# A four-layer graph network: one-hot spans of 128 nodes at multiples of 64, a ring of 44 chunks, and scores tied to a product

## The chip, the core and the metric

The kernel runs on one core of a Trainium2 chip. The metric is the device time of one execution in microseconds; three runs of the kernel before gave 4579.54, 4588.5 and 4594.84 us, so the median is 4588.5 us. The profile is of one further execution.

## What is computed

3125 nodes with 256 features pass four layers. Each adds the result of a graph step and of a dense mixer to the nodes, and then of a mixture of experts. The graph steps sum rows of their neighbours. 50000 edges, sorted by destination, serve layers 0, 1 and 3; layer 2 sums by the other end of the edge. The last mixture of experts has an attention over 32768 edges of its own.

```python
# layer 0 (layer 3 alike, without the relation types)
msgs = where(edge_type == r, x[src] @ rel_W[r], msgs)        # r = 0..3
agg  = segment_sum(msgs, dst);  deg = clip(segment_sum(1, dst), 1)
out  = relu(x @ self_W + self_b + agg / deg)
# layer 1: attention with 4 heads over the edges (the last experts' gates alike)
att   = leaky_relu(s_src[src] + s_dst[dst] + e_proj, 0.2)
exps  = exp(att - segment_max(att, dst)[dst])
alpha = exps / (segment_sum(exps, dst)[dst] + 1e-12)
out   = segment_sum(x_proj[src] * alpha, dst) + bias
# layer 2
agg   = segment_sum(A_values * h[col], row)
```

## The kernel before

**Chunks, tiles and one-hots.** Nodes lie in 25 tiles of 128. The 50000 edges lie in 391 chunks of 128, sorted by destination, so a tile takes about 16 chunks. For each chunk POOL issues an indirect DMA that gathers 128 rows of a table (L447, L842). DVE makes a one-hot matrix `E` from the edges' places `dl` (L416, L418): row = edge, column = node. PE multiplies it with the gathered rows and adds the result up in a PSUM tile `seg` (L430). `near` (L48) gives the tiles that chunk c may touch: one in the middle of a tile, two within three chunks of a boundary. A chunk with two tiles gets a one-hot of 256 columns and two products, one for each tile's own accumulator. After a tile's last product its `close` reads the sum from PSUM. The kernel first checks that the edges keep to these bounds (`regular`, L2370, and `route_check`, L2086, for the last attention); if they don't, a general path is taken instead.

**Gather loops.** `seg_near` (L434) serves layers 0, 2 and 3: gathers go to a ring of 16 buffers, and the products of chunk i - 12 are emitted after gather i. Layer 2 weights its one-hots. `gat_near` (L782) serves layer 1 and the tail. It has one ring of 35 chunks. Softmax works on batches of 16 chunks: `batch` adds gathered and stored scores (L806), takes running maxima over equal destinations along the edges (transposes by PE into `ga`, scans by DVE, L812 to L829), and writes `ex` by an exponential on ACT (L834). A batch starts 8 chunks after its last gather, and chunk i - 30 is scaled in place by `ex` (L854, DVE) and multiplied after gather i. A gather waits until the product of the chunk that had its buffer is done.

**What runs beside it.** Generators are interleaved by `drive`: three chunks of layer 0 to a step of its mixer, four of layer 1 to one step of its mixer, one of the layernorm and two of the edge scores, two of layer 3 to a step of its mixer, four of the tail to three steps of the experts. Within this a scheduler orders PE, DVE, ACT and SP at compile time; POOL keeps the order of emission. [...] 

**Names.** `mm` (L107) is the helper for dense products, `ps` takes a PSUM bank, `l1_edge_scores` (L1353) adds edge scores to `pre`, `gat_close` (L859), `l0_close` (L1027) and `l3_close` (L1755) finish a tile. `hb` (L1794) is the layernorm of layer 3's mixer.

Of the kernel before, what the change touches and what calls it, by code (L numbers as in the profile page):

```python
# [7 lines left out]
F32 = mybir.dt.float32  # L8
BF16 = mybir.dt.bfloat16
I32 = mybir.dt.int32  # L10
AF = mybir.ActivationFunctionType
# [24 lines left out]
AHEAD = 12  # L36
HALO = 40
CB = 16
RING = 35
T2 = 16  # L40
BIG = 2.0 ** 100

# [5 lines left out]
def near(c, nt=T):  # L48


    return range(max(0, (c - 3) >> 4), min(nt - 1, (c + 3) >> 4) + 1)


def lin_size(n):
# [10 lines left out]
def drive(*gens):  # L65

    live = list(gens)
    while live:
        for g in list(live):
            for _ in range(g[1]):  # L70
                try:
                    next(g[0])
                except StopIteration:
                    live.remove(g)
                    break
# [19 lines left out]
class Net:  # L95
    def __init__(self, tc, a, out):
        self.tc, self.nc, self.a, self.out = tc, tc.nc, a, out
        self.flip = 0
        self.apart = {}
        self.one_hots = 8  # L100
        self.pump = None


    def ps(self, n=512, name="mm", parts=P):
# [2 lines left out]
    def mm(self, out, pairs):  # L107
        last = len(pairs) - 1
        for i, (l, r) in enumerate(pairs):
            m = self.nc.tensor.matmul(out, l, r, start=(i == 0), stop=(i == last))  # L110
            if self.pump is not None:
                self.pump.after(m.ins, out.free_size())

# [308 lines left out]
    def to_tiles(self, pool, g, c, rows_c, A, w, close, weight=None):  # L422


        for t, e in self.one_hot(pool, g, c, weight):
# [5 lines left out]
            if last:  # L431
                close(t, A.pop(t))

    def seg_near(self, pool, g, table, gidx, close, count=False, ahead=AHEAD, weight=None):  # L434


        nc = self.nc
        n = g["n"]
        w = D + count
        ring = [pool.tile([P, w], F32, name=f"G{i}") for i in range(ahead + 4)]  # L440
        if count:
            for r in ring:
                nc.vector.memset(r[:, D:], 1.0)
        A = {}
        for i in range(n + ahead):
            if i < n:
                nc.gpsimd.indirect_dma_start(out=ring[i % len(ring)][:, :D], out_offset=None, in_=table,  # L447
                                             in_offset=bass.IndirectOffsetOnAxis(ap=gidx[:, i:i + 1], axis=0))
            c = i - ahead
            if c >= 0:  # L450
                self.to_tiles(pool, g, c, ring[c % len(ring)], A, w, close, weight)
            yield

    def table_sum(self, pool, ts, t0, n, out):
# [324 lines left out]
            v = pre[:, q * per:(q + 1) * per, :]  # L779
            self.evac(v, ps[q].rearrange("p (h c) -> p c h", h=4))  # L780

    def gat_near(self, pool, g, table, pre, pen, d, close):  # L782

        nc = self.nc
        n, late = g["n"], CB + 14
        f = d + 2
        nb = -(-n // CB)  # L790
        ring = pool.tile([P, RING, 4, f], F32, name="ring")
        att = pool.tile([P, nb * CB + 2, 4], F32, name="att")
        ex = pool.tile([P, nb * CB, 4], F32, name="ex")
        nc.vector.memset(att, 0.0)

        def spans(c0, c1):
            while c0 < c1:
                e = min(c1, c0 - c0 % RING + RING)
                yield c0, e, ring[:, c0 % RING:c0 % RING + e - c0]
                c0 = e  # L800

        def batch(b):
            c0 = b * CB
            lo, hi = (c0 + 1 if b else 0), min(c0 + CB + 1, n)
            for s, e, r in spans(lo, hi):
                nc.vector.tensor_add(att[:, s + 1:e + 1, :], r[:, :, :, d + 1], pre[:, s:e, :])  # L806
            v = att[:, lo + 1:hi + 1, :]
            nc.vector.scalar_tensor_tensor(v, v, 0.2, v, op0=OP.mult, op1=OP.max)
            yield
# [21 lines left out]
            qv = q.rearrange("p (j c h) -> p j c h", j=2, h=4)  # L831
            dif = pool.tile([P, CB, 4], F32, name="dif", bufs=2)
            nc.vector.tensor_sub(dif, att[:, c0 + 1:c0 + CB + 1, :], qv[:, 0])
            nc.scalar.activation(ex[:, c0:c0 + CB, :], dif, AF.Exp)  # L834
            for s, e, r in spans(c0, min(c0 + CB, n)):
                nc.vector.tensor_copy(r[:, :, :, d + 1], qv[:, 1, s - c0:e - c0, :])

# [1 line left out]
        live = []  # L839
        for i in range(n + late):  # L840
            if i < n:
                nc.gpsimd.indirect_dma_start(out=ring[:, i % RING].rearrange("p h f -> p (h f)"), out_offset=None,  # L842
                                             in_=table,
                                             in_offset=bass.IndirectOffsetOnAxis(ap=g["src"][:, i:i + 1], axis=0))
            for b in range(nb):
                if i == min(b * CB + CB, n - 1) + 8:
                    live.append(batch(b))
            for s in list(live):
                if next(s, self) is self:
                    live.remove(s)  # L850
            c = i - late
            if c >= 0:
                r = ring[:, c % RING]
                nc.vector.tensor_mul(r[:, :, :d + 1], r[:, :, :d + 1],  # L854
                                     ex[:, c, :, None].to_broadcast([P, 4, d + 1]))
                self.to_tiles(pool, g, c, r.rearrange("p h f -> p (h f)"), A, 4 * f, close)
            yield

    def gat_close(self, pool, table, d, aself, nodeg, eps, out):  # L859
# [1226 lines left out]
    def route_check(self, pool, table, ok):  # L2086

        nc = self.nc
        rec = self.load_all(pool, "rec6", table, 2)
        bad = pool.tile([P, 5], F32, name="rc_b")  # L2090
        nc.vector.memset(bad, 0.0)
        nc.vector.tensor_copy(bad[:, 4:5], self.beyond)
        dst = pool.tile([P, C2], F32, name="rc_d")
        far = pool.tile([P, C2], F32, name="rc_f")
        nc.vector.tensor_copy(dst, rec[:, :, 1])
        self.ordered(pool, dst, C2, self.dlin2, bad[:, 0:2])

        lo = self.first_nodes(pool, self.sixteenths(pool, "rc13", 13, C2))
        hi = self.first_nodes(pool, self.sixteenths(pool, "rc19", 20, C2))
        nc.vector.tensor_tensor(far, dst, lo, op=OP.is_lt)  # L2100
        nc.vector.tensor_reduce(bad[:, 2:3], far, axis=AX.X, op=OP.add)
        nc.vector.tensor_scalar(hi, hi, 128.0, float(T2 * P), op0=OP.add, op1=OP.min)
        nc.vector.tensor_tensor(far, dst, hi, op=OP.is_ge)
        nc.vector.tensor_reduce(bad[:, 3:4], far, axis=AX.X, op=OP.add)
        self.none_bad(pool, bad, ok)

    def l3_near_setup(self, keep, pool, table, penc):
# [4 lines left out]
        g["src"] = keep.tile([P, C2], I32, name="e2src")  # L2112
        g["dl"] = keep.tile([P, C2], F32, name="e2dl")
        nc.vector.tensor_copy(g["src"], rec[:, :, 0])
        nc.vector.tensor_sub(g["dl"], rec[:, :, 1], self.first_nodes(pool, self.sixteenths(pool, "ns", 13, C2)))
        w = self.load(pool, "wg", wtile(a["L3_ffn_W_gat"]))
        full = [P, T, 16]
        h = pool.tile(full, F32, name="h")
# [121 lines left out]
    def tail_regular(self, sorted_r):  # L2240
# [3 lines left out]
        with tp("g3") as gp, tp("ffn3") as fp, Banks(self, mm=4, ga=2, seg=2):  # L2244
# [21 lines left out]
                if t % 4 == 3:  # L2266
                    gate(t - 3, 4)
            close = self.gat_close(gp, rows_d, 4, aself, nodeg, 1e-16, out)
            drive((self.gat_near(gp, g, rows_d, pre, pen, 4, close), 4), (experts, 3))

    def tail_general(self):
        nc, tc, a = self.nc, self.tc, self.a
# [41 lines left out]
    def first_nodes(self, pool, lim):  # L2314

        v = pool.tile([P, lim.shape[1]], F32, name="lo128")
        self.nc.vector.tensor_scalar(lim, lim, 1.0, 1.0, op0=OP.max, op1=OP.subtract)
        self.nc.vector.tensor_scalar(v, lim, 128.0, None, op0=OP.mult)
        return v

    def ordered(self, pool, dstf, n, dlin, bad):

# [47 lines left out]
    def regular(self, pool, g):  # L2370


        nc = self.nc
        full = [P, C1]
        lim = [self.sixteenths(pool, f"rg_{base}", base) for base in (13, 3)]
        tf = self.bits(pool, g["dst"], "rg_t", 7)
        junk = pool.tile(full, F32, name="rg_j")
        bad = pool.tile([P, 5], F32, name="rg_b")
        nc.vector.memset(bad, 0.0)
        nc.vector.scalar_tensor_tensor(junk, tf, 1.0, lim[0], op0=OP.add, op1=OP.is_lt, accum_out=bad[:, 0:1])  # L2380
        nc.vector.scalar_tensor_tensor(junk, tf, 0.0, lim[1], op0=OP.add, op1=OP.is_gt, accum_out=bad[:, 1:2])
        self.dlin = self.dramk.tile([1, lin_size(C1)], F32, name="dlin")
        self.ordered(pool, g["dstf"], C1, self.dlin, bad[:, 2:4])

        self.sbase = self.keep.tile([P, T], F32, name="sbase")
        self.counts(pool, self.bits(pool, g["src"], "rg_k", 7), C1, T, self.sbase)
        self.uneven(pool, self.sbase, T, bad[:, 4:5])
        ok = pool.tile([P, 1], I32, name="rg_ok")
        self.none_bad(pool, bad, ok)

        g["dl"] = self.keep.tile(full, F32, name="e1dl")
        nc.vector.tensor_sub(g["dl"], g["dstf"], self.first_nodes(pool, lim[0]))
        return ok

    def fast(self):
# [3 lines left out]
        with tc.tile_pool(name="keepf", bufs=1) as keep, tc.tile_pool(name="dramf", bufs=1, space=DRAM) as dram:  # L2399
# [1 line left out]
            tp = lambda name: tc.tile_pool(name=name, bufs=1)  # L2401
            plain = dict(mm=6, acc=2)
            edges = dict(mm=3, acc=2, g=3)
            sums = dict(mm=3, acc=2, seg=3)


            self.deg2 = keep.tile([P, T], F32, name="deg2")
# [33 lines left out]
            with tp("att1") as gp:  # L2441
# [9 lines left out]
                def add_x(t, o):  # L2451
                    v = self.x[:, t, :].rearrange("p (h f) -> p h f", h=4)
                    nc.vector.tensor_add(v, v, o)
                    closed.add(t)
                with Banks(self, mm=1, acc=2, ga=2, seg=3), tp("mix1") as mp:
                    close = self.gat_close(gp, table, 64, aself, nodeg, 1e-12, add_x)
                    drive((self.gat_near(gp, g, table, pre, pen, 64, close), 4), (self.l1_mix_lean(mp), 1),
                          (self.norm_after(closed, self.mixed), 1), (self.l1_edge_scores(mp, pre, vb), 2))
            with Banks(self, **plain):
                route = tp("route")  # L2460
# [336 lines left out]
```

## Time and profile before

| | |
|---|---|
| median of three runs | 4588.5 us |
| the profiled execution | 4591.9 us |
| its span, first to last instruction | 4590.2 us |
| granted TensorE clock, mean | 0.859 |
| seg products of L430, `G` | 3210 records, 917.6 us busy |
| seg products of L430, `ring` | 1762 records, 424.5 us busy |
| one-hots of L416 | 1173, 365.1 us busy |

A product of fp32 stands in the trace as two records, so 4972 records are 2486 products: 535 for each of layers 0 to 3 and 346 in the tail. [...] the mean length of one record is longer than the time until the next starts. A row of the page's groups gives busy time, the mean of one, and the idle time of the engine before such instructions with its releasers. `G<-h_tab` are the gathers of layer 0, `ring<-l1rows` of layer 1, `G<-tab,e3src` of layer 2, `G<-tab,e1src` of layer 3, and `ring<-l3rows` of the tail.

### The profile page before, as it was taken

How to read it: one execution, taken by the hardware profiler on the slowest of the kernel's cores; microseconds unless marked ns; L12 is line 12 of the kernel's file. 1: busy time of each engine (PE TensorE's matmuls, PEld its weight loads, DVE VectorE, ACT ScalarE, POOL GpSimd, SP SyncE). 2: the span in 40 equal slices, each digit the busy share in tenths (PEclk: the TensorE clock that was granted, in tenths of full speed). 3: DMA queues.
4: the chain of work that ended last, by engine and by line, in shares of the span. 5: the costliest groups of instructions: out<-in, count | busy, mean ns of one | idle time of the engine just before them, and what ended most of it. 6: DMA issues, size and time to landing. Idle time of an engine off the chain costs nothing. (4 is left out here: it accounts for less than half of the span.)

```text
span 4590.2 us, 47080 instructions
## 1 busy us (share of the span) xinstructions
PE 3616.8 (79%) x13977; PEld 2403.7 (52%) x13977; DVE 2211.5 (48%) x7451; ACT 749.8 (16%) x1455; POOL 2612.1 (57%) x2605
## 2 busy tenths in 40 slices
PE   7889876954877867677777679998699995389898
PEld 3457543633545545455455334555476773257665
DVE  4477431145777775883545342113665233515443
ACT  2010001211100112113111011222122220013222
POOL 0577776755777747565777524770376565226550
PEclk9889977976978878788998868999799998588888
DMA  3433343314433420123333300001233233200000
GB/s 123 160 96 101 103 122 99 110 49 127 133 101 104 109 63 21 31 50 97 103 110 107 111 21 8 15 8 37 84 111 109 82 98 114 59 4 10 8 8 29
DMA packets 231200, 348.62 MB, mean 76 GB/s; under 512 B 74128, under 2 KB 168135, under 8 KB 230936
## 3 DMA queue, kind: packets, MB, share of 16 engines
q0 software_dynamic: 108384, 219.50, 17.5%
q1 hardware_dynamic: 118136, 121.97, 8.6%
q10 hardware_dynamic: 4416, 4.01, 0.3%
q8 instruction: 118, 1.93, 0.2%
q14 instruction: 146, 1.20, 0.1%
HBM read 294.62 MB, written 50.61 MB: 75 GB/s over the span
## 5 line engine op out<-in xcount | busy, mean ns | idle before, releaser
L430 PE MATMUL seg<-G,E 128*128 128x256 f32 (+1 forms) x3210 | 917.6, 417 | 217.0 <-DMA G<-tab,e3src 85.2
L430 PEld LDWEIGHTS seg<-G,E 128*128 128x128 f32 x3210 | 601.7, 202 | 500.9 <-issue 134.3
L110 PE MATMUL mm<-xnT,w 128*128 128x512 f32 (+1 forms) x1232 | 540.5, 586 | 20.9 <-DVE x L2226 20.5
L447 POOL DMA_INDIRECT G<-h_tab,gi x391 | 386.0, 987 | 264.7 <-DMA selfw<-in_L_gnn_self_W 136.9
L416 DVE TENSOR_SCALAR E<-iota_row,e1dl 128x128 f32<-128x128 f32 (+1 forms) x1173 | 365.1, 321 | 354.1 <-PE seg L430 343.5
L357 POOL DMA_INDIRECT by_src<-rec,place x391 | 419.3, 1073 | 188.9 <-PE mm L110 121.0
L447 POOL DMA_INDIRECT G<-tab,e1src x391 | 383.9, 982 | 202.6 <-PE seg L430 131.0
L842 POOL DMA_INDIRECT ring<-l1rows,e1src x391 | 423.6, 1083 | 132.0 <-issue 54.2
L447 POOL DMA_INDIRECT G<-tab,e3src x391 | 387.6, 991 | 123.3 <-PE seg L430 65.5
L430 PE MATMUL seg<-ring,E 128*128 128x264 f32 (+1 forms) x1762 | 424.5, 381 | 31.2 <-DVE E L416 21.2
L110 PE MATMUL mm<-w,hT 128*128 128x256 f32 (+1 forms) x1712 | 398.2, 385 | 0.5 <-ACT hT L1554 0.5
L357 POOL DMA_INDIRECT by_dst<-rec,place x256 | 251.5, 982 | 240.1 <-PE mm L110 196.0
L842 POOL DMA_INDIRECT ring<-l3rows,e2src x256 | 248.2, 970 | 225.8 <-PE seg L430 155.8
L430 PEld LDWEIGHTS seg<-ring,E 128*128 128x128 f32 x1762 | 309.5, 213 | 117.1 <-DVE E L416 47.5
L110 PEld LDWEIGHTS mm<-xnT,w 128*128 128x128 f32 x1232 | 236.9, 205 | 248.6 <-issue 217.8
L110 PEld LDWEIGHTS mm<-w,hT 128*128 128x128 f32 (+1 forms) x1712 | 319.0, 190 | 59.1 <-issue 16.9
L165 PE MATMUL mm<-ident,xn 128*128 128x128 f32 x400 | 95.1, 393 | 226.5 <-DVE xn L178 223.3
L418 DVE TENSOR_SCALAR E<-iota_row,e3dl,rec 128x128 f32<-128x128 f32 (+1 forms) x391 | 144.1, 381 | 218.9 <-PE seg L430 217.2
L1717 DVE SCALAR_TENSOR_TENSOR x<-mm,l2t_r,x 128x256 f32<-128x256 f32 x150 | 70.8, 482 | 299.7 <-PE mm L110 299.7
L165 PEld LDWEIGHTS mm<-ident,xn 128*128 128x128 f32 x400 | 65.9, 191 | 256.1 <-DVE xn L178 175.2
L854 DVE TENSOR_TENSOR ring<-ring,ex 128x260 f32<-128x260 f32 (+1 forms) x647 | 192.2, 319 | 2.4 <-ACT ex L834 2.3
L1710 ACT ACTIVATE h<-mm,b 128x512 f32<-128x512 f32 (+1 forms) x168 | 107.2, 641 | 361.2 <-PE mm L110 360.9
(710 smaller groups left out, 4962.5 us busy)
## 6 DMA issues: line engine op xcount, KB each, us to landing
w<-in_L_ffn_w SPq DMA_DIRECT2D x16, 1024.0 KB
h_tab<-htab_s SPq DMA_DIRECT2D x25, 512.0 KB
r_b<-rowa SPq DMA_DIRECT2D x64, 128.0 KB
bn_h<-c_h SPq DMA_DIRECT2D x50, 128.0 KB
G<-h_tab,gi POOLq DMA_INDIRECT x391
by_src<-rec,place POOLq DMA_INDIRECT x391
ring<-l1rows,e1src POOLq DMA_INDIRECT x391
G<-tab,e3src POOLq DMA_INDIRECT x391
```

The source lines that it names most:

```text
L110: m = self.nc.tensor.matmul(out, l, r, start=(i == 0), stop=(i == last))
L165: self.nc.tensor.transpose(p[:, i * P:(i + 1) * P], src(t0 + i)[:, k * P:(k + 1) * P], self.ident)
L357: return self.nc.gpsimd.indirect_dma_start(out=table, out_offset=bass.IndirectOffsetOnAxis(ap=idx, axis=0), in_=src, in_offset=None, bound ...
L416: self.nc.vector.tensor_scalar(e[:, :w], self.iota2[:, :w], g["dl"][:, c:c + 1], None, op0=OP.is_equal)
L418: self.nc.vector.tensor_scalar(e[:, :w], self.iota2[:, :w], g["dl"][:, c:c + 1], weight[:, c:c + 1], op0=OP.is_equal, op1=OP.mult)
L430: self.nc.tensor.matmul(A[t], e, rows_c, start=first, stop=last)
L447: nc.gpsimd.indirect_dma_start(out=ring[i % len(ring)][:, :D], out_offset=None, in_=table, in_offset=bass.IndirectOffsetOnAxis(ap=gidx[:, ...
L842: nc.gpsimd.indirect_dma_start(out=ring[:, i % RING].rearrange("p h f -> p (h f)"), out_offset=None, in_=table, in_offset=bass.IndirectOff ...
L854: nc.vector.tensor_mul(r[:, :, :d + 1], r[:, :, :d + 1], ex[:, c, :, None].to_broadcast([P, 4, d + 1]))
L1710: nc.scalar.activation(o[:, f, :n], p, AF.Relu, bias=b[:, 2 * e + f:2 * e + f + 1])
L1717: nc.vector.scalar_tensor_tensor(self.x[:, t, :], p, r[:, t, e:e + 1], self.x[:, t, :], op0=OP.mult, op1=OP.add)
```

## The change

The sums of layers 0, 1, 3 and the tail go by windows in place of tiles. Window k spans the 128 nodes from 64 k. Chunk c belongs to window `ts[0] + ts[-1]`: an even window is a tile, an odd one the second half of one tile and the first half of the next. So each chunk has one one-hot of 128 columns and one product. When a window ends, ACT copies it out of PSUM, an even one whole, an odd one in two halves; DVE adds the half windows of both sides to the tile, and `close` now reads this tile in SBUF. `dl` is counted from the window's first node, and the checks are written for windows. The sums' `seg` banks go from three to two, and `mm` gets one more, in layers 0 and 1.

Layer 1's ring goes from 35 to 44 chunks. Its scores are emitted 12 chunks after a batch's last gather (8 before) and its products 34 chunks behind the gathers (30 before); the tail keeps 35, 8 and 30. In both, the addition of scores gets a dependency on the product that was emitted last, so it waits for it on the chip. `ex` becomes three rotating tiles, one for each batch.

```diff
-RING = 35
+RING = 44
+def window(c, nt=T):
+    ts = near(c, nt)
+    return ts[0] + ts[-1]
...
     def mm(self, out, pairs):
...
             m = self.nc.tensor.matmul(out, l, r, start=(i == 0), stop=(i == last))
+            self.product = m.ins
...
+    def to_windows(self, pool, g, c, rows_c, A, w, close):
+        nc, nt = self.nc, g["tiles"]
+        k = window(c, nt)
+        t = k // 2
+        e = pool.tile([P, P], F32, name="E", bufs=self.one_hots)
+        nc.vector.tensor_scalar(e, self.iota_row, g["dl"][:, c:c + 1], None, op0=OP.is_equal)
+        if c == 0 or window(c - 1, nt) != k:
+            A["sum"] = self.ps(w, name="seg")
+        last = c == g["n"] - 1 or window(c + 1, nt) != k
+        self.product = nc.tensor.matmul(A["sum"], e, rows_c, start=(c == 0 or window(c - 1, nt) != k), stop=last).ins
+        if not last:
+            return
+        acc = A.pop("sum")
+        if k % 2 == 0:
+            A["own"] = pool.tile([P, w], F32, name="W_own", bufs=2)
+            nc.scalar.copy(A["own"], acc)
+        else:
+            if t == 0:
+                A["side"] = pool.tile([P, w], F32, name="W_side", bufs=2)
+                nc.vector.memset(A["side"][:64], 0.0)
+            side, A["side"] = A["side"], pool.tile([P, w], F32, name="W_side", bufs=2)
+            nc.scalar.copy(side[64:], acc[:64])
+            nc.scalar.copy(A["side"][:64], acc[64:])
+            own = A.pop("own")
+            nc.vector.tensor_add(own, own, side)
+            close(t, own)
+        if k == 2 * (nt - 1):
+            own = A.pop("own")
+            nc.vector.tensor_add(own[:64], own[:64], A.pop("side")[:64])
+            close(t, own)
...
-                self.to_tiles(pool, g, c, ring[c % len(ring)], A, w, close, weight)
+                if weight is None:
+                    self.to_windows(pool, g, c, ring[c % len(ring)], A, w, close)
+                else:
+                    self.to_tiles(pool, g, c, ring[c % len(ring)], A, w, close, weight)
...
-    def gat_near(self, pool, g, table, pre, pen, d, close):
+    def gat_near(self, pool, g, table, pre, pen, d, close, size, wait):
-        n, late = g["n"], CB + 14
+        n, late = g["n"], CB + wait + 6
...
-                nc.vector.tensor_add(att[:, s + 1:e + 1, :], r[:, :, :, d + 1], pre[:, s:e, :])
+                v = nc.vector.tensor_add(att[:, s + 1:e + 1, :], r[:, :, :, d + 1], pre[:, s:e, :])
+                self.tc.add_manual_dep(v.ins, self.product.name, info, reason="not ahead of its gathers")
...
-                if i == min(b * CB + CB, n - 1) + 8:
+                if i == min(b * CB + CB, n - 1) + wait:
                     live.append(batch(b))
...
+    def windows(self, pool, name, n, nt):
+        a = self.sixteenths(pool, name + "_wa", 13, n)
+        b = self.sixteenths(pool, name + "_wb", 3, n)
+        self.nc.vector.tensor_scalar(a, a, 1.0, 1.0, op0=OP.max, op1=OP.subtract)
+        self.nc.vector.scalar_tensor_tensor(a, b, float(nt - 1), a, op0=OP.min, op1=OP.add)
+        self.nc.vector.tensor_scalar(a, a, 64.0, None, op0=OP.mult)
+        return a
...
-            sums = dict(mm=3, acc=2, seg=3)
+            sums = dict(mm=4, acc=2, seg=2)
...
-                with Banks(self, mm=1, acc=2, ga=2, seg=3), tp("mix1") as mp:
+                with Banks(self, mm=2, acc=2, ga=2, seg=2), tp("mix1") as mp:
-                    drive((self.gat_near(gp, g, table, pre, pen, 64, close), 4), (self.l1_mix_lean(mp), 1),
+                    drive((self.gat_near(gp, g, table, pre, pen, 64, close, RING, 12), 4), (self.l1_mix_lean(mp), 1),
```

## The prediction

> **What bounds the kernel now.** I read the page's engine totals first, then the windows of each gather stage, then the groups of gathers and products, then the waits of the two stages where something moves. Stages, by the first and last gather in the timeline: layer 0 from 148.7 to 661.6 us, layer 1 from 1090.4 to 1644.3, layer 2 (not changed) from 2099.7 to 2605.2, layer 3 from 3277.2 to 3862.6, the tail's attention from 4001.5 to 4474.3. Below: the page's totals; four windows (length, then busy time and count of PE, PEld, DVE, ACT, POOL, granted clock, DMA share, GB/s); three groups (busy, mean ns of one, idle before them by releaser); one gather of the timeline; POOL's waits from 3500 to 3750 and DVE's from 1150 to 1660 (us, times, longest).
>
> ```profile
> PE 3616.8 (79%) x13977; PEld 2403.7 (52%) x13977; DVE 2211.5 (48%) x7451; ACT 749.8 (16%) x1455; POOL 2612.1 (57%) x2605
> 550.00:600.00 50.00, 42.28 (x149) 29.54 (x149) 18.50 (x61) 1.36 (x5) 37.81 (x41) 0.82 0.36 105
> 1090.00:1650.00 560.00, 413.28 (x1608) 275.33 (x1608) 409.68 (x1380) 59.20 (x110) 423.68 (x392) 0.81 0.42 115
> 3500.00:3750.00 250.00, 250.00 (x992) 186.13 (x991) 67.37 (x210) 67.33 (x110) 133.58 (x141) 1.00 0.29 83
> 4050.00:4517.00 467.00, 437.16 (x1912) 313.00 (x1912) 195.14 (x1016) 115.96 (x170) 211.59 (x221) 0.89 0.07 7
> ...
> L447 POOL DMA_INDIRECT G<-h_tab,gi x391 | 386.0, 987 | 264.7 <-DMA selfw<-in_L_gnn_self_W 136.9 <-PE seg L430 58.2 <-issue 47.2
> L447 POOL DMA_INDIRECT G<-tab,e1src x391 | 383.9, 982 | 202.6 <-PE seg L430 131.0 <-issue 37.9 <-PE mm L110 17.9
> L842 POOL DMA_INDIRECT ring<-l1rows,e1src x391 | 423.6, 1083 | 132.0 <-issue 54.2 <-PE seg L430 39.0 <-DVE ring L854 5.8
> ...
> 1395.45 0.95 POOL L842 DMA_INDIRECT ring<-l1rows,e1src  x1 [0.30 <-issue]
> ...
> POOL G L447 <- PE seg L430: 87.5, 60, 4.3
> ...
> DVE att L806 <- DMA ring<-l1rows,e1src: 76.3, 19, 11.0
> ```
>
> A gather takes 0.95 us on POOL and 0.30 pass before the next: 1.25 us, or 40 in 50 us, which is the 41 of the layer 0 window. So a stage of 391 gathers cannot be shorter than its POOL durations plus 390 gaps of 0.305 (119 us). What a stage loses beyond that is idle minus 119: layer 0 264.7 - 136.9 (before its first gather) - 119 = 9 us; layer 1 132.0 - 119 = 13; layer 3 202.6 - 119 = 83. Products of layers 0 and 1 are therefore hidden behind POOL. In layer 3 PE is busy for 250.00 of 250 us from 3500, with 141 gathers where 199 would fit; the POOL waits of that window name the seg products (87.5 us). That stretch is PE-bound. In the tail PE is busy 437 of 467 us, but the chain that ended last passes through landings of `ring<-l3rows` too, so that is PE-bound with handovers.
>
> [...] each product stands as two records, and in dense stretches of the timeline a record starts every 0.216 us at 256 columns and 0.429 at 512. So a seg product of 256 columns costs 0.43 us. [...] Layer 1, with most DVE work, has the longest gathers (1083 ns against 982 to 991)[...].
>
> **The change part by part.**
>
> Windows. Of 391 chunks 144 lie within 3 chunks of a tile boundary (6 at each of 24) and have two products; now each has one. The tail drops 6 x 15 = 90. Layer 2 keeps its weighted form.
>
> Layer 3, PE-bound stretch 3500 to 3750: the groups count 384 seg records, 192 products, for about 140 chunks: 52 go, 52 x 0.43 = 22 us, all on the path since PE never idles there. Before 3500 POOL lost only 83 - (117.7 of idle in that window - 141 x 0.305 = 75) = 8 us, so no more than 8 to 9 can come from there; part of it is layernorm work on DVE (PE waited 7.9 us for `hb` between 3450 and 3500), but PE enters the stretch nearly that much earlier. After 3750 POOL sets the pace, no gain. Sum 31; from 20 (PE is held by the mixer) to 45.
>
> Layer 0: 9 us lost, at two places. In the order of the new program PE has 25 products ahead of the mixer's first, where it had 19 chunks. The mixer then begins about 5 us later, and seg 25 comes about 5 us after gather 41 wants its buffer (16 in the ring), against the 3.25 us POOL lost there before. Fewer products later give it back. Value 0, from -6 to +6.
>
> Layer 1: the ring of 44 takes away POOL's wait when the ring first fills (9.0 us at 1140, the longest) and a later one of 3.5: up to 13. The second mm buffer lets the edge-score chain (mm, ACT copy, transposes, about 3.5 us a step at 1120 to 1147) overlap with itself, so the first scores are not later, although the order puts ten of its additions ahead of the first scaling where there were eight. I take 10. Scores 12 chunks behind, on a product emitted earlier, replace DVE's 76.3 us of waits for gathers by short waits for PE; DVE was busy 409.68 of 560 us, so this slack is not the path: 0. The relation of scores to scaling is the same (late minus wait was 22 and is 22), so the end of the stage keeps its 22 us from last gather to last product.
>
> Tail: 22 records of 24 columns took 2.57 us up to the next product's start, 0.117 each, so 90 products cost 21 us. PE was busy 94% of the window, but part of the seg work lies in stretches where PE waits for gathers; I take two thirds, 14, from 5 to 21. The tie moves the first score product behind more expert products, which PE has to do anyway: 0.
>
> Closing. Each window now leaves PSUM by an ACT copy (0.37 us for a 256-column ACT copy out of PSUM), odd ones by two, and each tile adds a DVE addition (0.42). ACT was busy 16%; in the new order no copy stands behind an ACT instruction that needs a later product than its own window's, and a bank is wanted again only 6 to 10 chunks later (over 7 us): 0 inside a stage. At the end of layers 0, 1 and 3 copy, addition and handover are on the path, 1 us each: -3; in the tail at four handovers to the experts, about 0.5 each: -2. The one-hot of a boundary chunk falls from 358 to 299 ns (144 x 0.06 = 9 us of DVE a layer), which pays the 25 x 0.42 = 10 us of additions. The additions and the closing products, formerly from PSUM, now take both inputs from SBUF[...]: layer 1 has 410 us of DVE work and about 40 us of excess duration, so 25 x 2 x 0.42 = 21 us bring about 2; from 0 to -6 for layers 0 and 1.
>
> Setup. `windows` is one more iota and a few operations on 128 x 391 or 128 x 256 (0.2 to 0.4 us each), in place of about as many: 0, at most -2.
>
> Sum: 0 + 31 + (10 - 2) + 14 - 3 - 2 = 48 us. The profiled execution took 4591.9 us (span 4590.2), so 4544; the median of the three runs is 3.4 below it, so **4540.5**.
>
> **The rivals.**
> 1. Gathers pace more than I think (12%): the mixer's own DVE and ACT steps hold PE in layer 3 when products go, half of 31 stays, and the tail, coupled to gathers, gains 3. For: PE waits for `hb`; against: no PE wait at all from 3500 to 3750. 48 - 15 - 11 = 22 us off: 4566.
> 2. The gain is larger (17%): layer 1's gathers shorten too because DVE no longer bunches its work after stalls (20 of its 40 us of excess), and the tail gives its whole 21. 48 + 20 + 7 = 75 off: 4513. For: 1083 against 987 ns; against: the amount of DVE work is the same.
> 3. Slower (12%): the tie in layer 1. The score addition heads DVE's queue and waits for PE; behind it stand the one-hots and scalings that PE needs next, so the two take turns. DVE idles 150 us in the window, 6 us for each of 25 batches. If a batch costs more than that, each further us costs 25: it passes the gain at 8 us a batch; at 9 it gives 75 - 48 = 27 slower, 4615. Against: the product named is seven chunks before the batch and is done within about 1 us of its one-hot.
> 4. No difference (3%): two stages swallow the gain by a new wait, 4588.
>
> **How the numbers follow.** My forecast has 56%, own range 4522 to 4560. What the measurement can tell from no change is 0.3%, 14 us. Faster: 56 + 12 + 17 = 85%; same 3%; slower 12%. A range that leaves out the slower case and the far end of the larger gain: 4505 to 4572.
>
> **What would show it.** Right: seg records fall from 4972 to 3928 (522 products gone, two records each), layer 3's gathers ending some 30 us sooner after their start (585 to about 555), layer 1's idle before gathers near 120 in place of 132.0, its longest wait at the start gone, layer 0 at 510 to 516. PE still full in the middle of layer 3. Wrong: DVE `att` waits on PE above 6 us a batch, PE waits on ACT copies of windows, POOL waits in layer 1 above 13 us, or mean gather duration in layer 1 above 1.1 us.

## The result, and the profile after

Four runs of the changed kernel gave 4511.75 to 4525.15 us, median 4520.4. The kernel before, run beside it, gave 4584.2. The ratio is 0.9856 (95% interval 0.983 to 0.9881): 64 us, where 48 were forecast. The time lies 20 us under the forecast 4540.5, just outside the forecast's own range of 4522 to 4560 and inside the wider 4505 to 4572. The profiled execution took 4522.75 us (span 4520.7, before 4590.2), and the difference of the two spans, 69.5 us, can be split by stage. Lengths are from the first to the last gather, for the tail from its first gather to the end of the span.

| stage | before | after | gain | forecast |
|---|---|---|---|---|
| layer 0 | 512.9 | 512.4 | 0.5 | 0 |
| layer 1 | 553.9 | 552.4 | 1.5 | 8 |
| layer 2 | 505.5 | 505.6 | -0.1 | 0 |
| layer 3 | 585.4 | 561.3 | 24.1 | 31 |
| tail, with its end | 588.7 | 542.1 | 46.6 | 12 |
| between the stages | | | -3.1 | -3 |

So the sum came out near the forecast, but not by its terms: the tail gave four times what it was given, and layers 1 and 3 less. Each column is one execution, and small gains in it are not sure. The profiles of the experiments below tell how far a stage differs where its code is the same. Layer 0 took 511 to 514 us in the three with the old one, 512 to 518 in the eleven with the new one; layer 1 547 and 554 as it was, 550 to 555 in the four with all of its changes; layer 3 584 to 586 and 557 to 561; the changed tail 540 to 548. So layer 3 won about 26 us and the tail some 46. Layer 1 is not shown to have won anything, and layer 0 lost 2 or 3 us if it changed at all.

The page's totals and the rows of the gathers (busy, mean ns of one, idle before them by releaser), all stages of the kernel after:

```profile
PE 3501.4 (77%) x12933; PEld 2226.3 (49%) x12933; DVE 2206.9 (49%) x7540; ACT 853.0 (19%) x1730; POOL 2613.5 (58%) x2606
...
L891 POOL DMA_INDIRECT ring<-l1rows,e1src x391 | 435.4, 1113 | 119.2 <-issue 67.4 <-PE seg L453 26.2 <-DMA ring<-l1rows,e1src 7.9
...
L488 POOL DMA_INDIRECT G<-tab,e1src x391 | 383.9, 982 | 178.4 <-PE seg L453 108.2 <-issue 36.1 <-PE mm L116 19.2
```

PE's count fell by 1044 records, which are the 522 products. Layer 1's idle is 119.2 us, the bare gap between gathers, so no wait for the ring is left; but the gathers' own time rose from 423.6 to 435.4 us, 12 of the 13 us won. In layer 3 the idle fell from 202.6 to 178.4.

Where layer 3 won is seen in three stretches, cut within two gathers of the same places as in the kernel before (windows of the kernel after: length, then busy time and count of PE, PEld, DVE, ACT, POOL, clock, DMA share, GB/s):

```profile
3279.00:3502.00 223.00, 189.75 (x787) 126.66 (x786) 154.15 (x468) 57.74 (x134) 166.00 (x162) 0.86 0.40 117
3502.00:3730.00 228.00, 227.70 (x891) 166.64 (x890) 63.23 (x220) 77.04 (x137) 133.43 (x141) 1.00 0.32 92
3730.00:3841.00 111.00, 81.28 (x253) 47.75 (x252) 38.62 (x134) 21.85 (x59) 84.18 (x89) 0.86 0.41 118
```

The middle stretch has the 141 gathers of the 250 us shown before, PE is as full as it was, and it takes 228 (227.0 between the 161st gather and the 301st, formerly 249.4): the 52 products at 0.43 (two records each, one starting every 0.216 us; the mean length of one in the kernel before is 417 ns). Ahead of it only 2 us were won (the 161st gather starts 220.5 us into the layer, formerly 222.6), behind it nothing.

What happened in the tail is seen in DVE's queue. Its start in the kernel before, DVE's timeline (start, duration, engine, line, operation, idle before it):

```profile
4027.63 0.28 DVE L806 TENSOR_TENSOR att<-ring,pre 128x68 f32<-128x68 f32 x1 [9.97 <-DMA ring<-l3rows,e2src]
4027.94 0.23 DVE L808 SCALAR_TENSOR_TENSOR att<-att 128x68 f32<-128x68 f32 x1
4047.60 0.27 DVE L806 TENSOR_TENSOR att<-ring,pre 128x64 f32<-128x64 f32 x1 [19.43 <-DMA ring<-l3rows,e2src]
4047.90 0.23 DVE L808 SCALAR_TENSOR_TENSOR att<-att 128x64 f32<-128x64 f32 x1
4050.01 0.17 DVE L806 TENSOR_TENSOR att<-ring,pre 128x8 f32<-128x8 f32 x1 [1.89 <-DMA ring<-l3rows,e2src]
4050.10 1.65 DVE L2226 SCALAR_TENSOR_TENSOR x<-mm,r,x 128x256 f32<-128x256 f32 x4
```

and PE's at the same place:

```profile
4026.99 7.07 PE L110 MATMUL mm<-w,hT 128*128 128x256 f32 x32
4050.63 10.16 PE L110 MATMUL mm<-xnT,w 128*128 128x512 f32 x16 [16.57 <-DVE x L2226]
```

The scheduler had put the scores of the first two batches, and of the third batch's first two chunks (128x8), ahead of the experts' `x` additions in DVE's queue. The second batch's scores waited 19.43 us for gathers and the third's 1.89; the `x` additions, whose products PE had ended by 4034.1, stood behind them with four `mm` banks in their hands: DVE began the first at 4050.10, after the last of those scores, and PE waited 16.57 us for one of those banks. In the kernel after (score addition L853, `x` addition L2269), PE at the corresponding place:

```profile
4009.84 7.03 PE L116 MATMUL mm<-xnT,w 128*128 128x512 f32 x16
4016.71 7.07 PE L116 MATMUL mm<-w,hT 128*128 128x256 f32 x32
```

and DVE, when the first scores come up:

```profile
4068.72 0.48 DVE L2269 SCALAR_TENSOR_TENSOR x<-mm,r,x 128x256 f32<-128x256 f32 x1 [10.69 <-PE mm L116]
4069.12 0.27 DVE L853 TENSOR_TENSOR att<-ring,pre 128x68 f32<-128x68 f32 x1
```

The tie forbids the scores to start before a product of the experts. PE runs through (no idle time stands in its two rows), and when the first scores come up, 90.5 us after the tail's first gather in place of 26.2, the gathers have long landed: they wait for nothing. Over the whole tail, up to its last gather, DVE's waits of `att` for landings (us, times, longest) were, before and after:

```profile
DVE att L806 <- DMA ring<-l3rows,e2src: 81.6, 18, 19.4
DVE att L853 <- DMA ring<-l3rows,e2src: 1.1, 2, 0.9
```

Whether this, or the fewer products, made the tail short, is what the experiments were to tell.

### The profile page after: what moved, and what is told of

It is laid out like the page before. It is cut to its first block, busy times and chain, and to the rows that moved or that the text cites. A ratio compares the mean times of both kernels' runs of the same rounds, so it can differ in the third digit from the quotient of the medians.

```text
span 4520.7 us, 45234 instructions
## 1 busy us (share of the span) xinstructions
PE 3501.4 (77%) x12933; PEld 2226.3 (49%) x12933; DVE 2206.9 (49%) x7540; ACT 853.0 (19%) x1730; POOL 2613.5 (58%) x2606
## 4 chain that ended last, share of the span: by engine, by line
PE 58%; DVE 18%; DMA 13%; issue 6%; POOL 2%; ACT 1%; SPq 0%; another core or an unknown queue 0%; POOLq 0%; DVEq 0%; ACTq 0%
PE mm L116 37%; PE seg L453 10%; DMA G<-tab,e3src 5%; PE seg L437 4%; DMA G<-h_tab,gi 3%; DMA ring<-l1rows,e1src 2%; DVE E L449 1%; DMA G<-tab,e1src 1%; PE mm L172 1%; DVE ln_st L181 1%; DVE ring L903 1%; POOL G L488 1%; DVE xn L185 1%; DVE r_m L2121 1%; PE mm L1411 1%
## 5 line engine op out<-in xcount | busy, mean ns | idle before, releaser
L453 PE MATMUL seg<-G,E 128*128 128x257 f32 (+1 forms) x1564 | 506.6, 448 | 136.3 <-DMA G<-h_tab,gi 66.1
L488 POOL DMA_INDIRECT G<-h_tab,gi x391 | 380.1, 972 | 269.7 <-DVE so_cum L693 136.4
L891 POOL DMA_INDIRECT ring<-l1rows,e1src x391 | 435.4, 1113 | 119.2 <-issue 67.4
L449 DVE TENSOR_SCALAR E<-iota_row,e1dl 128x128 f32<-128x128 f32 x1173 | 336.6, 301 | 326.4 <-PE seg L453 311.2
L488 POOL DMA_INDIRECT G<-tab,e1src x391 | 383.9, 982 | 178.4 <-PE seg L453 108.2
L453 PEld LDWEIGHTS seg<-G,E 128*128 128x128 f32 x1564 | 303.2, 214 | 317.2 <-DVE E L449 106.9
L453 PE MATMUL seg<-ring,E 128*128 128x264 f32 (+1 forms) x1294 | 360.3, 408 | 96.0 <-DVE E L449 55.1
L437 PE MATMUL seg<-G,E 128*128 128x256 f32 x1070 | 329.4, 431 | 112.2 <-DMA G<-tab,e3src 80.2
L453 PEld LDWEIGHTS seg<-ring,E 128*128 128x128 f32 x1294 | 223.7, 218 | 205.7 <-DVE E L449 114.8
L437 PEld LDWEIGHTS seg<-G,E 128*128 128x128 f32 x1070 | 200.4, 207 | 232.0 <-DMA G<-tab,e3src 73.3
```

What stands on the lines that cost most here:

```text
L437: self.nc.tensor.matmul(A[t], e, rows_c, start=first, stop=last)
L449: nc.vector.tensor_scalar(e, self.iota_row, g["dl"][:, c:c + 1], None, op0=OP.is_equal)
L453: self.product = nc.tensor.matmul(A["sum"], e, rows_c, start=(c == 0 or window(c - 1, nt) != k), stop=last).ins
L891: nc.gpsimd.indirect_dma_start(out=ring[:, i % size].rearrange("p h f -> p (h f)"), out_offset=None, in_=table, in_offset=bass.IndirectOff ...
```

## The experiments

### The tie in the tail

Two theories: the tie made the tail short (T), or the windows did (W). In the changed kernel it was left out in the tail alone:

```diff
-                self.tc.add_manual_dep(v.ins, self.product.name, info, reason="not ahead of its gathers")
+                if size == RING: self.tc.add_manual_dep(v.ins, self.product.name, info, reason="not ahead of its gathers")
```

> The changed kernel with the tie (the dependency of the score addition on the product emitted last) left out in the tail only; layer 1 keeps it. Theory T, the tie made the tail faster than predicted: the score additions of the first batch stand on DVE ahead of the 16 x updates of the experts again and wait there for their gathers, PE waits 14 to 18 us for x at the start of the tail, the tail's gathers last 442 to 450 us in place of 427, and the time is 15 to 22 us above the changed kernel (4535 to 4543). Theory W, the windows alone did it (fewer products, less PE time): the tail stays at 425 to 430 us, and the time within 4 us of the changed kernel's 4520.

Measured: 4558.75 us, ratio to before 0.9934 (0.992 to 0.9947), 38 us slower than the changed kernel (32 when each is compared with the kernel before that ran beside it). The tail took 591.6 us in place of 542.1. DVE's waits in it (us, times, longest):

```profile
DVE x L2269 <- PE mm L116: 137.2, 58, 10.1
DVE att L853 <- DMA ring<-l3rows,e2src: 84.7, 16, 19.5
```

and PE's:

```profile
PE mm L116 <- DVE x L2269: 18.8, 2, 17.3
PE ga L860 <- DVE att L856: 14.6, 3, 10.2
PE ga L860 <- DVE g_mx L2239: 10.6, 1, 10.6
PE seg L453 <- DVE ring L903: 10.4, 3, 5.8
```

The 19 us wait of DVE at the start is back, PE waits 17.3 us for `x` there, and three more kinds of wait come with it, of which the changed kernel has 0.4 us in all: the transposes of scores (`ga`) now stand ahead of experts' products in PE's queue, and PE stood before them. Theory T was right in kind and half as large as the truth.

The same from the other side, the kernel before with the tie alone, in the tail alone:

```diff
+            self.product = m.ins
...
+                if d == 4:
+                    info = mybir.DependencyInfo(mybir.DependencyClass.Sync, mybir.DependencyReason.DATA)
+                    self.tc.add_manual_dep(v.ins, self.product.name, info, reason="not ahead of its gathers")
```

> The kernel before with the tie alone, and that in the tail only. Theory T: the wait of 16.6 us of PE for x at the start of the tail goes, the tail's gathers last 450 to 460 us in place of 473, and the time falls by 13 to 22 us (4563 to 4572). Theory W: the tail stays at 470 to 476 and the time within 4 us of the kernel before (4580 to 4588).

Measured: 4556.7 us, ratio 0.9938 (0.9924 to 0.9951), the tail 559.6 us in place of 588.7. DVE's waits of `att`, now short and for PE:

```profile
DVE att L807 <- PE mm L110: 22.6, 7, 4.7
```

So one added dependency is worth about half of the whole change. The four tails, each of one profiled execution:

| tail, us | without the tie | with the tie | the tie |
|---|---|---|---|
| tiles | 588.7 | 559.6 | 29.1 |
| windows | 591.6 | 542.1 | 49.5 |
| the windows | -2.9 | 17.5 | |

In these profiles the windows pay in the tail only when the tie is there: without it PE's waits on queued-up scores swallow the 90 products. The times of all executions do not bear this out. In their medians the tie alone gives 33.5 us, the change without it in the tail 31.5, and both 64, so as far as the times can tell they add. The profile with tiles and tie is of the fastest of five executions, the one with windows and no tie of the slowest of five, and the same tail differs by up to 8 us between profiles. That the two parts depend on each other is therefore not shown.

The account of the differences in the table is PE's idle and busy time. PE's waits in the set-up of the scores (`mm` for `se`, 43.8 us in all four) are left out. From tiles without the tie to tiles with it, its other waits go from 44.7 to 21.9 us (up to the last gather) and its busy time, to the end, from 509.5 to 503.1. With windows they go from 61.6 to 25.6 and from 494.2 to 481.5. The products are the same with and without the tie; the longer busy time goes with a lower granted clock (0.85 against 0.89 with windows, 0.87 against 0.90 with tiles), of which the last section says more.

Does it take a tie, or would later emission do? The tail without it, with its scores emitted 12 chunks after the last gather of a batch and a ring of 43:

```diff
-gat_near(gp, g, rows_d, pre, pen, 4, close, 35, 8)
+gat_near(gp, g, rows_d, pre, pen, 4, close, 43, 12)
```

> The changed kernel without the tie in the tail, but with the tail's ring at 43 chunks and its scores emitted 12 chunks behind. If what counts is only that gathers have landed when the scores are emitted: DVE's waits of att for landings fall below 20 us, the tail's gathers last 415 to 432, time 4512 to 4524. If the scores' place in DVE's queue counts, which the compile-time scheduler chooses without the tie: waits of att for landings stay above 50 us, the tail's gathers last 455 or more, time 4540 to 4560.

Measured: 4559.25 us, tail 584.7 us. DVE's waits of `att` for landings, up to the last gather:

```profile
DVE att L853 <- DMA ring<-l3rows,e2src: 91.3, 13, 19.4
```

Emitting later took none of these waits away. The first scores start 26.1 us after the first gather, as in the other two kernels without the tie (26.2), where with it they start 91.0 us (tiles) and 90.5 us (windows) after it. So it is the place in the queue that counts, and without a dependency the scheduler chose the same early place. By what estimate it does so is not shown.

With the tie kept and the tail at 44 and 12:

```diff
-gat_near(gp, g, rows_d, pre, pen, 4, close, 35, 8)
+gat_near(gp, g, rows_d, pre, pen, 4, close, 44, 12)
```

> The changed kernel with the tail's ring at 44 chunks and its scores 12 chunks behind, as layer 1 has them. Theory: with the tie PE is the bound in the tail, a longer ring only lets POOL run ahead: the tail from first gather to span's end stays at 540 to 546 us, time within 4 us of 4520. Rival, PE still waits for scores that come late: tail 5 to 15 us shorter, time 4505 to 4515.

Measured: 4517.7 us (0.9822 to 0.9881 of before), the same as the changed kernel within its interval; the tail 541.4 us. The gathers end 12 us sooner, and nothing after them does: PE is the bound.

### Layer 1: who lengthens the gathers

The sum of layer 1's gather durations was 423.6 us in the profile of before and 418.6 in that of the run with the tie in its tail, whose layer 1 is the same; 435.4 in the changed kernel, and 432.2, 435.1 and 437.7 in the three runs above that kept its layer 1. So some 14 us are real, at a spread of about 5 between profiles of the same code. Each part of the change that touches layer 1 was undone by itself, first the tie:

```diff
-                self.tc.add_manual_dep(v.ins, self.product.name, info, reason="not ahead of its gathers")
+                if size == 35: self.tc.add_manual_dep(v.ins, self.product.name, info, reason="not ahead of its gathers")
```

> The changed kernel with the tie left out in layer 1 only. DVE's waits of att for landings come back (50 us or more in layer 1). If the tie is what moved DVE's work onto the gathers in layer 1: the sum of gather durations falls from 435 to about 424, the stage from 552 to 540-545 us, the time to 4508-4513. If not (ring or windows did it): sum 432 to 438, stage 550 to 556, time within 4 us of the changed kernel's 4520. If the tie was needed there: POOL waits beyond 119 of idle, stage over 558.

then the ring and the emission:

```diff
-gat_near(gp, g, table, pre, pen, 64, close, RING, 12)
+gat_near(gp, g, table, pre, pen, 64, close, 35, 8)
```

> The changed kernel with layer 1's ring back at 35 chunks and its scores 8 chunks behind; all else stays. Ring theory (gathers got longer because POOL no longer stalls, so that more of them meet DVE's long operations): idle before layer 1's gathers rises from 119 to 128-134, the sum of their durations falls from 435 to 422-428, stage 551 to 557, time within 4 us of the changed kernel. Windows theory (the additions and closings from SBUF lengthen the gathers): the sum stays at 432 to 438, so the stage is 560 to 567 and the time 8 to 14 us above the changed kernel's 4520.

then the windows, with the one-hot of a boundary chunk made from the window's `dl`:

```diff
-        if weight is None:
+        if weight is None and len(ts) == 2:
+            self.nc.vector.tensor_scalar(e, self.iota2, 64.0, g["dl"][:, c:c + 1], op0=OP.subtract, op1=OP.is_equal)
+        elif weight is None:
...
-                self.to_windows(pool, g, c, r.rearrange("p h f -> p (h f)"), A, 4 * f, close)
+                if d == 64:
+                    self.to_tiles(pool, g, c, r.rearrange("p h f -> p (h f)"), A, 4 * f, close)
+                else:
+                    self.to_windows(pool, g, c, r.rearrange("p h f -> p (h f)"), A, 4 * f, close)
```

> The changed kernel with layer 1's sums by tiles again (two products and a one-hot of 256 columns for a boundary chunk, close reads PSUM); ring of 44, tie and banks stay as in the changed kernel. Windows theory (additions and closings with both inputs in SBUF lengthen layer 1's gathers): the sum of their durations falls from 435 to 418-425 at an idle of 119-120, the stage from 552 to 536-544 us, and the time by 8 to 15 us to 4505-4512. Rival, the banks or the different timing lengthen them: sum 431 to 438, stage 549 to 556, time within 4 us of 4520.

and last the shares that `Banks` gives out, eight in all in layer 1 of either kernel, and on the kernel before the reverse:

```diff
-                with Banks(self, mm=2, acc=2, ga=2, seg=2), tp("mix1") as mp:
+                with Banks(self, mm=1, acc=2, ga=2, seg=3), tp("mix1") as mp:
```

> The changed kernel with layer 1's banks as before (one for mm, three for seg). Bank theory: sum of layer 1's gather durations 419 to 427 in place of 435, stage 538 to 546 us, time 4506 to 4514. Rival, banks do not matter: sum 431 to 438, stage 550 to 557, time within 4 us of 4520.

> The kernel before with the changed bank shares of layer 1 alone (two banks for mm, two for seg). Bank theory (with a second mm buffer the edge scores and the mixer run earlier, and DVE's long operations fall on the gathers): the sum of layer 1's gather durations rises from 419-424 to 430-436, and with the first wait for the ring still there the stage to 558-568; time 4590 to 4602. Rival, banks do not matter: sum 417 to 426, stage 546 to 555, time within 4 us of the kernel before.

The medians, and layer 1's gathers and length in one profile each:

| run | us | ratio to before, interval | gather durations | idle before | stage |
|---|---|---|---|---|---|
| changed kernel | 4520.4 | 0.983 to 0.9881 | 435.4 | 119.2 | 552.4 |
| without the tie in layer 1 | 4522.6 | 0.9842 to 0.9872 | 437.0 | 120.3 | 555.5 |
| ring 35, scores 8 behind | 4523.6 | 0.9848 to 0.9884 | 434.6 | 130.0 | 562.5 |
| layer 1 by tiles | 4519.6 | 0.9829 to 0.9878 | 436.0 | 125.2 | 559.6 |
| banks of layer 1 as before | 4516.7 | 0.9825 to 0.9873 | 431.0 | 119.2 | 548.0 |
| kernel before, new banks | 4593.1 | 0.9997 to 1.0019 | 434.1 | 128.9 | 561.3 |

None of tie, ring and windows is needed for the longer gathers: with any one of them undone the gathers are as long. The ring does what it was for (10 us of idle come back without it), and the windows save 6 us of idle. The new bank shares alone lengthen the gathers of the kernel before by 10 to 15 us, as much as the whole change, but this is one profile, of the slowest of twelve executions, and the median time rose by only 4.7 us, with 1 inside the ratio's interval. Taken out of the changed kernel, they give back only 4, no more than the spread. So the banks seem to suffice, but are not needed: with them gone, something else of the change still costs about 10 us. Which, and whether two parts act together, stays open.

What the added time consists of can be seen in the trace of the kernel after. The 60 gathers of layer 1 under which DVE did nothing took 0.95 us, none over 1.00. The 42 that took over 1.5 us hold 43 of the 66 us that all 391 took beyond 0.945 each; before the change there were 29 such gathers, with 29 of 54 us. So the rise is one of long gathers under DVE work. A piece of it, POOL:

```profile
1402.96 0.95 POOL L891 DMA_INDIRECT ring<-l1rows,e1src  x1 [0.30 <-issue]
1404.21 1.30 POOL L891 DMA_INDIRECT ring<-l1rows,e1src  x1 [0.30 <-PE ga L877]
1405.82 3.31 POOL L891 DMA_INDIRECT ring<-l1rows,e1src  x1 [0.30 <-DMA ring<-l1rows,e1src]
```

and DVE at the same time:

```profile
1403.20 1.49 DVE L1446 TENSOR_TENSOR xh<-xh,hs 128x1280 f32<-128x1280 f32 x1
...
1405.80 1.48 DVE L1450 TENSOR_TENSOR kv<-xh,rb_L_mix_kln_weight 128x1280 f32<-128x1280 f32 x1
1407.21 1.10 DVE L903 TENSOR_TENSOR ring<-ring,ex 128x260 f32<-128x260 f32 x3
1408.23 0.27 DVE L449 TENSOR_SCALAR E<-iota_row,e1dl 128x128 f32<-128x128 f32 x1
1408.42 0.42 DVE L903 TENSOR_TENSOR ring<-ring,ex 128x260 f32<-128x260 f32 x1
1408.76 0.41 DVE L449 TENSOR_SCALAR E<-iota_row,e1dl 128x128 f32<-128x128 f32 x1
1408.96 0.42 DVE L903 TENSOR_TENSOR ring<-ring,ex 128x260 f32<-128x260 f32 x1
```

A gather that takes 0.95 us when it is alone took 3.31 under the last eight DVE operations shown, which follow each other without a pause; six of them read two tensors in SBUF. But the gather at 1402.96 lay for 0.7 us under the long operation of L1446, which reads two tensors as well, and took 0.95. So lying under such an operation does not by itself make a gather long, and what decides stays open. To measure the effect as a whole, 192 additions were put into layer 1, once with both inputs in SBUF, once with one in PSUM (`acc` in place of the `own` that is read in the added line):

```diff
             nc.vector.tensor_add(own, own, side)
+            for _ in range(8 if w == 264 else 0):
+                nc.vector.tensor_add(side, own, side)
```

> The changed kernel with 8 further additions of 128x264 to each of 24 tiles of layer 1, both inputs in SBUF, into a buffer that is no longer read: 192 x 0.42 = 81 us more of DVE. If such additions lengthen gathers: at the share of the changed kernel's own (1.1 of 7.4 us that they lie over gathers) the sum of gather durations rises by 9 to 14 us, to 444 or more, and the stage to 562 or more. If they don't (DVE has the room, gathers don't care): sum 432 to 438, stage 550 to 557, time within 4 us of 4520.

> As the run with 8 further additions in layer 1, but one of the two inputs is the window's sum in PSUM. Theory of the two inputs in SBUF: gathers are not lengthened, sum 432 to 438 where the run with SBUF inputs shows 444 or more, and this run is 8 to 14 us faster than that one. Rival, any DVE work over gathers lengthens them: both runs show the same sum within 3 us.

Measured: 4540.7 us (0.9866 to 0.9932 of before) and 4528.3 (0.9845 to 0.9893). The gathers' rows of the page, first SBUF:

```profile
L893 POOL DMA_INDIRECT ring<-l1rows,e1src x391 | 452.7, 1158 | 119.5 <-issue 67.6
```

then PSUM:

```profile
L893 POOL DMA_INDIRECT ring<-l1rows,e1src x391 | 447.4, 1144 | 119.1 <-issue 69.2
```

Idle stays at the bare gap, so no wait explains it; the gathers themselves get 17 and 12 us longer for 82 us of added DVE work. Both inputs in SBUF are worse, if at all, by 5 us, as much as profiles of the same code differ, and the two runs' intervals of time overlap; the expectation that PSUM inputs cost nothing failed. Measured by this, the 25 additions that the windows bring cost 25/192 of 17, or 2 us.

### Old banks and longer tail ring together

Banks of layer 1 as before and the tail at 44 and 12:

```diff
-                with Banks(self, mm=2, acc=2, ga=2, seg=2), tp("mix1") as mp:
+                with Banks(self, mm=1, acc=2, ga=2, seg=3), tp("mix1") as mp:
...
-gat_near(gp, g, rows_d, pre, pen, 4, close, 35, 8)
+gat_near(gp, g, rows_d, pre, pen, 4, close, 44, 12)
```

> The changed kernel with layer 1's banks as before and the tail's ring at 44 chunks with scores 12 chunks behind. If the bank theory holds, layer 1's stage is 538 to 546 and the tail's gathers some 12 us shorter as with the longer ring alone: 4495 to 4510. If banks do not matter: 4510 to 4520.

Measured: 4513.9 us, ratio 0.9832 (0.9808 to 0.9855), the lowest of all, but its interval overlaps the changed kernel's: not shown to be better. Layer 1 took 548.6 us, the tail also 548.6.

## Why the prediction was right, and where it was wrong

The direction was right, and so was the size, but the size in good part by luck: a term put at nothing, the tie in the tail, gave about half of what was measured, and terms put too high in layers 1 and 3 made up for part of it. Without the tie in the tail the same change gave 31.5 us in place of the 48 forecast.

**Layer 3's PE-bound stretch** was right: 52 products, 22 us forecast and 22.4 measured, and PE full before and after. The other 9 us of the sum ("no more than 8 to 9 can come from there") measured 2: ahead of the stretch PE already waited for `hb` and one-hots, so products taken out there only let it wait longer (PE's waits for one-hots between the layer's start and 3500 rose from 3.0 to 11.1 us). An upper bound was entered as a value.

**Layer 1.** The idle side was right: the ring took away the wait when it first fills, 132.0 to 119.2. The term "from 0 to -6", taken as -2 for longer gathers, was mis-sized: 12 us in this profile, about 14 over all of them. The additions for which it was reckoned do cost about 2, estimated from the added ones (25/192 of 17). What was left out is that another part of the change could lengthen the gathers too: the bank shares seem to, and with them gone some 10 us are still there. Layer 1 has no slack for that, as POOL sets its pace: its idle of 119.2 us is the bare gap. With gathers this much longer, layer 1 is not shown to have won anything where 8 us were forecast. The forecast's own sign for this, a mean above 1.1 us, did appear (1.113). The sentence that the tie would "replace DVE's 76.3 us of waits for gathers by short waits for PE" was wrong for layer 1: 70.3 us of waits for landings are still there, beside 1.9 for PE. Its product lies 34 chunks behind the gathers and the scores' last gather 12 behind, so the product is done long before those gathers have landed. These waits cost nothing, as said: without the tie in layer 1 the time is the same.

**The tail.** The step that failed is "The tie moves the first score product behind more expert products, which PE has to do anyway: 0". It looked at what the tie puts behind PE, and not at what stood behind the scores on DVE. The trace of before had the answer, and the forecast even named the chain's "landings of `ring<-l3rows`": 81.6 us of DVE waits for landings in the tail, and PE's 16.6 us for `x` at its start. It priced such waits only in layer 1, as free, since DVE had slack there and POOL was the bound. In the tail the instructions behind the wait feed the engine that is the bound, and there DVE's wait became PE's: 19.43 and 1.89 us of the one, 16.57 of the other. Measured, the tie is worth 33.5 us in the median time on tiles and 32 to 38 on windows (29.1 and 49.5 in single profiles of the tail).

The windows' term in the tail, 14 minus 2, measured 17.5 with the tie and -2.9 without, in single profiles; as the median times of the two parts add, such a difference is not shown, and the true size of this term stays open between the two.

**Layer 0, closings, setup.** Layer 0 came out at 0.5 us, but not quite as forecast: its first stall grew to 7.5 us and the idle as a whole by 5.5, and what paid for it were gathers 5.9 us shorter in sum (386.0 to 380.1), not the products that are gone. In the ten other profiles with this layer 0 it took 512.8 to 517.6 us, so it may have lost 2 or 3, inside the forecast's range of 6. Between the stages 3.1 us were lost (1.7 after layer 0, 2.5 after layer 1, about 1 won elsewhere) where 3 were reckoned.

**The rivals.** The slower one, scores in layer 1 that take turns with PE, did not occur: DVE's waits of `att` for PE in layer 1 are 1.9 us in all. The larger gain is nearest in time (its 4513), but half of its mechanism, shorter gathers in layer 1, is the opposite of what happened; the other half, the tail's products in full, came near in the profiles with the tie (17.5 of 21). Gathers that pace more explain layer 3's 24 in place of 31 in part, but not in the way described there: the PE-bound stretch lost nothing.

## What to carry to other kernels

A wait at the head of a queue is judged by what stands behind it: find the instructions that come next on that engine and ask whether they feed the engine that bounds this very stage. The answer can differ between two stages that run the same code: here 19.43 us of DVE's wait made PE wait 16.57 in the tail, and 70.3 us of such waits in layer 1 cost nothing. Where a scheduler places an instruction that depends only on DMAs, emitting it later need not move it (26.1 us after the first gather, 26.2 without), while a dependency on a product of the bounding engine did (90.5). When two parts are tried together and apart, compare the times of many executions before you say that they depend on each other: single profiles of the same stage differ by several us (the changed tail took 540 to 548).

## What the runs showed of the hardware

Layer 1's gathers of 128 rows got longer when 192 additions, 82 us of DVE in all, were put beside them: by 12 us in sum with one input in PSUM (447.4 against 435.4) as well as by 17 with both in SBUF (452.7), in one profile each, at a spread of about 5 between profiles of the same code. What makes a single gather long was not shown: the one at 1405.82 took 3.31 us under DVE operations that mostly read two tensors in SBUF, and the one at 1402.96 took 0.95 with 0.7 us of L1446, which reads two as well. The additions may act through the timing of other DVE work, which these runs don't separate.

In the tail of the kernel before, a wait of PE cost more than its length. The two PE rows of the tail's start show it: the 16 records of 512 columns that came after the wait of 16.57 us took 10.16 us, the same 16 without a wait before them in the kernel after 7.03, at a granted clock of 1.00. Before the wait, from 4026.99 to 4034.06, the clock granted to TensorE was 1.00 too; after it, it stands in windows of the same trace (length, then busy time and count of PE, PEld, DVE, ACT, POOL, clock, DMA share, GB/s):

```profile
4050.60:4056.70 6.10, 6.07 (x7) 2.52 (x8) 1.15 (x3) 0.69 (x1) 0.00 (x0) 0.50 0.00 0
4056.80:4060.60 3.80, 3.80 (x10) 1.67 (x9) 0.00 (x0) 1.37 (x2) 0.00 (x0) 1.00 0.00 0
```

For 6.1 us after the wait the clock was at 0.50, then at 1.00, and half of the 6.1 is the 3.1 us by which the row is longer. What sets the length of such a stretch was not shown. Over the tail, the same products were busy for 12.7 us less with the tie than without it on windows, and 6.4 us less on tiles, at a higher granted clock (0.89 against 0.85, and 0.90 against 0.87). The forecast had no such term.
